# A transformer block with adaptive norms: second norm tile by tile behind the projection, inverse roots by Newton steps on VectorE

## The chip, the cores and the metric

The kernel runs on one core of a Trainium2 chip. The metric is device time in microseconds (us); smaller is better. TensorE is called PE in the profile, VectorE DVE, ScalarE ACT, GpSimd POOL, and the engine that issues most DMAs SP.

## The reference

One block of a transformer over x of 8 x 1024 x 512 in float32, with a condition vector of 512 per batch element:

```python
mod = jax.nn.silu(condition) @ Wada + bada
sh_a, sc_a, gt_a, sh_m, sc_m, gt_m = jnp.split(mod, 6, axis=1)
xn = _layernorm(x, g1, be1)
xm = xn * (1.0 + sc_a[:, None, :]) + sh_a[:, None, :]
x = x + gt_a[:, None, :] * _attention(xm, Wqkv, Wproj, bproj)   # 16 heads, causal
xn = _layernorm(x, g2, be2)
xm = xn * (1.0 + sc_m[:, None, :]) + sh_m[:, None, :]
h = jax.nn.gelu(xm @ W1 + b1, approximate=False)
x = x + gt_m[:, None, :] * (h @ W2 + b2)
```

`_layernorm` takes mean and variance over the 512 features of a row and multiplies by one over the root of the variance plus 1e-5. The hidden layer has 2048 features.

## The kernel before, in words

The 8 x 1024 rows are 16 blocks of 512 rows (two per batch element); a block is four tiles of 128 rows. Each block goes through these steps: norm and modulation ("a"), projections k, q and v, attention in four groups of four heads, output projection with the residual add (`project_out`), norm and modulation ("m"), four `up` steps with GELU, four `down` parts and the second residual add. Products of 512 x 512 are made from seven products of halves (`strassen`), with sums of halves of weights kept in DRAM.

The order of all engines' queues is written out when the kernel is built. A planner keeps one clock per engine (`now`, lines 94 to 141). Each instruction is issued together with a `note` that books its engine for so many ns, and records when its results are due (`written`) and its inputs free (`left`). `linear` walks through the steps of `plan` as one thread of TensorE work, side threads (`start`) run beside it, and attention (`attend`) takes TensorE by turns with them: `step_aside` lets linear work run until the tile that attention needs is due, and `work` advances the thread whose needs are due first. Work of VectorE and ScalarE that can wait stands in lists (`jobs`, `act_jobs`, `pool_jobs`) and is issued when the planner's clocks say that it is due. `either` chooses VectorE or GpSimd for an elementwise operation, `sooner` VectorE or ScalarE.

In PSUM, TensorE has one tile of four banks for scores ("sc", L1541; emptied by VectorE with the mask add L1553 and the row maxima L1556) and for weights of attention ("st", L1620 and L1632; emptied by ScalarE's exponential L1644), a bank for the weighted sum of values ("po", L1672), and three banks for all linear products (L202) and transposes (L735), emptied by VectorE (L193, L185, L739) or ScalarE (L188, L745). GpSimd sums the attention weights (L1762), masks them (L1649) and splits the maxima into bfloat16 parts (L1575 to L1578; VectorE in some cases).

A norm (`normalize`, L580) has four statistics on VectorE (`bn_stats`, `bn_aggr`: L590, L591), booked 850 ns each, and then, once for all four tiles, `power` on GpSimd (L611 to L616): variance plus eps, the power -1/2, and the offset, booked 1500. The normalized tile ("hat") is then made by VectorE or ScalarE (L626, L631). The first two blocks' first norm uses a root on ScalarE and a reciprocal (`root`), and the last block's second norm goes tile by tile through ScalarE (`normalize_tile`). In `project_out` (L1013) the product of each tile is multiplied by the gate row into y (L1044), added to the residual by `add_to` (L1054, issued at L158 on VectorE or L161 on GpSimd), and after the fourth tile `normalize` is called (L1061). `modulated` then transposes the normalized tiles on TensorE (L735) for the keys in `by_pe`, which are a0, a1 and every m; the other keys go through `turn`, by block transposes on VectorE (L671) and DRAM.

Of the kernel before, what the change touches and what calls it, by code (L numbers as in the profile page):

```python
# [8 lines left out]

F32 = mybir.dt.float32  # L10
BF16 = mybir.dt.bfloat16
AF = mybir.ActivationFunctionType
ALU = mybir.AluOpType
AX = mybir.AxisListType
# [3 lines left out]
EPS = 1e-5  # L18
# [4 lines left out]
def kernel(  # L23
# [36 lines left out]
    P = 128  # L60
# [51 lines left out]
    def note(engine, ns, reads=(), writes=(), port=False):  # L112
        start = max(now[engine], due(reads, writes))
        if port:
            start = max([start] + [b for a, b in pool_spans if a <= start < b])
        end = start + ns
        now[engine] = end
        if engine == "POOL":
            pool_spans.append((start, end))
            del pool_spans[:-16]  # L120
        for k in reads:
            left[k] = max(left.get(k, 0.0), end + SYNC)
        for k in writes:
            written[k] = end + SYNC
        return end
# [275 lines left out]
    nc.gpsimd.memset(eps, EPS)  # L401
    ones = const.tile([P, hd], F32, tag="ones", name="ones")
    nc.gpsimd.memset(ones, 1.0)
    minus_half = const.tile([P, NTT], F32, tag="minus_half", name="minus_half")
    nc.gpsimd.memset(minus_half, -0.5)
    minus_ones = const.tile([P, P], BF16, tag="minus_ones", name="minus_ones")
    nc.gpsimd.memset(minus_ones, -1.0)
    mcols = const.tile([P, NTT, P], BF16, tag="mcols", name="mcols")
# [116 lines left out]
    def add_job(job, reads, first=False):  # L525

        at = sum(1 for other in jobs if other[2]) if first else len(jobs)
        jobs.insert(at, (job, reads, first))
# [48 lines left out]

    hats = {}

    def normalize(tiles, key, sources):  # L580

        for t in range(NTT):
            written["hat", key, t] = NEVER
        mv = small.tile([P, NTT, 2], F32, tag="mv", name=f"mv_{key}")
        rstd = small.tile([P, NTT], F32, tag="rstd", name=f"rstd_{key}")
        offset = small.tile([P, NTT], F32, tag="offset", name=f"offset_{key}")

        def statistics(t):
            st = small.tile([P, nc.vector.BN_STATS_DIM], F32, tag="st", name=f"st_{key}_{t}")
            nc.vector.bn_stats(st, tiles[:, t, :])  # L590
            nc.vector.bn_aggr(mv[:, t, :], st)  # L591
            note("DVE", 850, [sources[t]], [("mv", key)])
            if t < NTT - 1:
                return
            if alone[0]:
                root()
                for i in range(NTT):
                    apply_tile(i)
                return
            power()  # L600
            for i in range(NTT):
                act_jobs.append((lambda i=i: apply_tile(i), [("rstd", key)]))

        def root():
            nc.scalar.activation(rstd, mv[:, :, 1], AF.Sqrt, bias=eps)
            note_act(300, "sqrt", [("mv", key)], [("rstd", key)])
            nc.vector.reciprocal(rstd, rstd)
            nc.vector.scalar_tensor_tensor(offset, mv[:, :, 0], -1.0, rstd, ALU.mult, ALU.mult)
            note("DVE", 360, [("rstd", key)], [("rstd", key)], port=True)

        def power():  # L611
            nc.gpsimd.tensor_scalar(rstd, mv[:, :, 1], EPS, None, ALU.add)
            nc.gpsimd.tensor_tensor(rstd, rstd, minus_half, ALU.pow)
            nc.gpsimd.tensor_scalar(offset, mv[:, :, 0], -1.0, None, ALU.mult)
            nc.gpsimd.tensor_tensor(offset, offset, rstd, ALU.mult)
            note("POOL", 1500, [("mv", key)], [("rstd", key)])  # L616

        to = [None]

        def apply_tile(t):  # L620
            if t == 0:
                hats[key] = to[0] = hat_tile(key) if key[0] == "m" else tiles
            xh, xt = to[0][:, t, :], tiles[:, t, :]
            reads, writes = [("rstd", key)], [("hat", key, t)]
            if (key == "a0" and t % 2) if alone[0] else sooner(reads, writes, 700, 800) == "DVE":
                nc.vector.tensor_scalar(  # L626
                    xh, xt, rstd[:, t : t + 1], offset[:, t : t + 1], ALU.mult, ALU.add
                )
                note("DVE", 700, reads, writes, port=True)
            else:  # L630
                nc.scalar.activation(  # L631
                    xh, xt, AF.Identity, bias=offset[:, t : t + 1], scale=rstd[:, t : t + 1]
                )
                note_act(800, None, reads, writes)

        for t in range(NTT):
            add_job(lambda t=t: statistics(t), [sources[t]], key[0] == "m")

    def normalize_tile(xt, key, t, source):

# [22 lines left out]
    def turn(key, rows, xm):  # L663

        small_blocks = xm.rearrange("p c n -> p (c n)")
        by_tile = small_blocks.rearrange("p (m h t i) -> p h m t i", m=NTT, h=NC, t=NTT)
        written["blocks", key] = NEVER

        def turn_tile(t):
            into = by_tile[:, :, :, t, :]  # L670
            nc.vector.transpose(into, rows[:, t, :].rearrange("p (h m i) -> p h m i", m=NTT, i=Q))  # L671
            done = [("blocks", key)] if t == NTT - 1 else []
            note("DVE", 620, [("hat", key, t)], done)

        for t in range(NTT):
            add_job(lambda t=t: turn_tile(t), [("hat", key, t)], key[0] == "m")
        yield [("blocks", key)], []
        held = kept.tile([P, NTT * D], F32, tag=f"held_{turns[0] % 2}", name=f"held_{key}")
        turns[0] += 1
        nc.sync.dma_start(held, small_blocks)  # L680
        written["held", key] = now["PE"] + HOLDING
        yield [("held", key)], []
        for m in range(NTT):
            some = held[:, ts(m, D)].rearrange("(a i) d -> i a d", i=Q)
            nc.sync.dma_start(rows[ts(m, Q), :, :], some)
        written["turned", key] = now["PE"] + HOLDING
        yield [("turned", key)], []
# [4 lines left out]
    def modulated(key, gain, shift, b, guards):  # L692
        for t in ("B11", "B21", "B22", "T1", "T2", "T3", "T4"):
            written[key, t] = NEVER
        turned = key not in by_pe
        if turned:
            yield [*(("hat", key, t) for t in range(NTT)), *guards], []
        else:
            yield [("hat", key, 0), *guards], [BANK]
        got = hats.pop(key)  # L700
# [309 lines left out]
    def add_to(xt, other, reads, writes, op=ALU.add):  # L1010
        either(xt, xt, other, op, [*reads, *writes], writes)

    def project_out(n):  # L1013
        at = take(NC)
        yield [("attended", n), ("xr begun", n)], []
        attT = qTs[n]
        tiles = [residual[n][:, t, :] for t in range(NTT)]
        last = n == NB - 1
        begun = []

        def begin(t):

            bank = yield from accumulate(
                [(attT[:, c, ts(t, P)], piece(at[c])) for c in range(NC - 1)], [("att", n)], False
            )
            begun.append(bank)

        for t, xt in enumerate(tiles):
            if last:
                while len(begun) <= max(t, 1):  # L1030
                    yield from begin(len(begun))
                bank = begun[t]
                yield [("att", n, t)], []
                matmul(
                    banks[bank], attT[:, NC - 1, ts(t, P)], piece(at[NC - 1]), False, True,
                    [("att", n, t)], bank,
                )
            else:
                bank = yield from accumulate(
                    [(attT[:, c, ts(t, P)], piece(at[c])) for c in range(NC)], [("att", n)]  # L1040
                )
            y = tmp.tile([P, D], F32, tag="y", name=f"y_{n}_{t}", bufs=2)
            ky = y_key("proj", True)
            combine_out(y, bank, banks[bank], gate_rows["ga"], [("row", "ga")], [ky], ALU.mult)  # L1044
            if last:
                run_pool_jobs(True)
                nc.vector.tensor_tensor(xt, xt, y, ALU.add)
                note("DVE", 700, [ky, ("xr", n, t)], [("xr", n, t)], port=True)
                following = normalize_tile(xt, f"m{n}", t, ("xr", n, t))
                if t > 0:  # L1050
                    pending()
                pending = following
            else:
                add_to(xt, y, [ky], [("xr", n, t)])  # L1054
        if last:
            pending()
        release(*at)
        run_pool_jobs(True)
        bias_row(n, "m")
        if not last:  # L1060
            normalize(residual[n], f"m{n}", [("xr", n, t) for t in range(NTT)])  # L1061

    def up(step):
        _, n, q = step
# [874 lines left out]
```

## Time and profile before

| | us |
|---|---|
| median of 3 runs | 3546.16 (3545.45 to 3546.95) |
| the profiled execution's own time | 3542.2 |
| its span, first to last instruction | 3540.5 |
| PE busy | 3482.5 (98%) |
| DVE busy | 2174.2 (61%) |
| POOL busy | 2074.9 (59%) |
| ACT busy | 1190.1 (34%) |

The profile is of one execution. Busy times are of each engine's own instructions, waits left out; the mean clock that the throttle granted to TensorE was 0.998 of full. A group row reads: line, engine, operation, output and inputs by the program's names, shapes and count; then busy time, mean ns of one, and the engine's idle time just before, with what ended it. A row of waits reads: who, on whom, total us, times, longest.

### The profile page before, as it was taken

Reading aid. Unit: us, or ns where it says so; the run is one execution under the profiler, and the core shown is the slowest. Engines: PE = TensorE matmul, PEld = TensorE weight load, DVE = VectorE, ACT = ScalarE, POOL = GpSimd, SP = SyncE. Lnnn points to the kernel's source line nnn. Section 1 sums busy time; section 2 is a strip of 40 time slices with the busy share of each in tenths; the row PEclk is TensorE's granted clock in tenths of the full one; section 3 lists DMA queues with packets and bytes.
Section 4 is the critical chain, followed back from the end, with each engine's and each line's share of the span. In section 5 each row is a group of like instructions: output and inputs, shape, how many; then the busy total and the mean of one; then the engine's idle time right before and its main releaser. Section 6 shows DMA issues by size and latency. Waiting matters only on the chain.

```text
span 3540.5 us, 120499 instructions
## 1 busy us (share of the span) xinstructions
PE 3482.5 (98%) x54621; PEld 1738.0 (49%) x54621; DVE 2174.2 (61%) x2383; ACT 1190.1 (34%) x1237; POOL 2074.9 (59%) x2249
## 2 busy tenths in 40 slices
PE   8999999999999999999999999999999999999999
PEld 4444445445554555545554454544545445454445
DVE  5776675564756557565675656656566556655563
ACT  2334323352333513235232342323423234232521
POOL 2667836666376664666546675366762667526660
PEclk9999999999999999999999999999999999999999
DMA  6753434335443354524445334443344533443334
GB/s 198 245 163 103 137 117 140 111 111 156 117 148 103 110 160 117 168 85 126 142 118 159 103 115 141 124 149 107 118 132 127 156 106 119 135 126 124 100 110 140
DMA packets 319555, 465.96 MB, mean 132 GB/s; under 512 B 26300, under 2 KB 176636, under 8 KB 316996
## 3 DMA queue, kind: packets, MB, share of 16 engines
q1 hardware_dynamic: 318928, 458.22, 42.9%
q8 instruction: 430, 7.05, 0.8%
q14 instruction: 81, 0.66, 0.1%
q10 hardware_dynamic: 116, 0.03, 0.0%
HBM read 412.99 MB, written 43.06 MB: 129 GB/s over the span
## 4 chain that ended last, share of the span: by engine, by line
PE 88%; DMA 4%; DVE 3%; POOL 2%; issue 1%; ACT 1%; SPq 0%; ACTq 0%; DVEq 0%; POOLq 0%
PE bank L202 61%; PE sc L1541 8%; PE po L1672 7%; PE st L1632 7%; PE st L1620 3%; DMA w<-in_L_cond_Wproj_dram 2%; PE bank L1693 2%; PE bank L735 1%; DVE mx L1556 1%; POOL pT L1762 1%; DMA w<-in_L_cond_Wada_dram 1%; PE bank L1594 0%; POOL hT L161 0%; POOL xr L161 0%; DVE sc L1553 0%
## 5 line engine op out<-in xcount | busy, mean ns | idle before, releaser
L1762 POOL TENSOR_TENSOR pT<-pT,pT 128x256 f32<-128x256 f32 (+3 forms) x1254 | 1207.2, 998 | 347.9 <-PE po L1672 181.4
L1644 ACT ACTIVATE pT<-st 128x2048 f32<-128x2048 f32 x288 | 541.0, 1879 | 1000.5 <-PE st L1632 883.3
L202 PE MATMUL bank<-w,hT 128*32 128x256 f32 x14336 | 812.3, 380 | 1.1 <-ACT rec L1702 0.9
L1556 DVE TENSOR_REDUCE mx<-sc 128x4 f32<-128x2048 f32 (+3 forms) x384 | 666.0, 1755 | 197.7 <-PE sc L1541 191.6
L202 PEld LDWEIGHTS bank<-w,hT 128*32 128x32 f32 x14336 | 450.4, 110 | 369.2 <-issue 81.4
L202 PE MATMUL bank<-xm_m,w 128*32 128x256 f32 x8192 | 499.6, 381 | 0.0
L202 PE MATMUL bank<-t_m,w 128*32 128x256 f32 x6144 | 381.2, 380 | 0.0
L1649 POOL TENSOR_SCALAR_AFFINE_SELECT pT<-pT 128x512 f32<-128x512 f32 x256 | 168.8, 677 | 346.6 <-ACT pT L1644 344.2
L202 PEld LDWEIGHTS bank<-xm_m,w 128*32 128x32 f32 x8192 | 255.7, 110 | 224.7 <-issue 62.4
L1553 DVE TENSOR_TENSOR sc<-sc,mask 128x1024 f32<-128x1024 f32 (+1 forms) x160 | 162.9, 1018 | 319.7 <-PE sc L1541 242.5
L1541 PE MATMUL sc<-kT,qT 32*128 32x512 f32 (+3 forms) x3072 | 329.1, 520 | 1.8 <-DVE mx L1556 1.1
L1672 PE MATMUL po<-pT,v 128*32 128x512 f32 (+3 forms) x3048 | 302.9, 492 | 2.0 <-POOL pT L1649 2.0
L1632 PE MATMUL st<-qT,kT 32*128 32x512 f32 (+3 forms) x3072 | 301.0, 487 | 0.0
L202 PEld LDWEIGHTS bank<-t_m,w 128*32 128x32 f32 x6144 | 190.0, 110 | 173.3 <-issue 48.5
L202 PE MATMUL bank<-xm_a,w 128*32 128x256 f32 x3968 | 249.3, 382 | 0.0
L202 PE MATMUL bank<-w,qT 128*32 128x512 f32 x2048 | 238.2, 594 | 8.7 <-DMA w<-in_L_cond_Wproj_dram 7.2
L1711 DVE RECIPROCAL rec<-rec 128x128 f32<-128x128 f32 x256 | 225.7, 920 | 31.5 <-ACT rec L1702 31.5
L1541 PEld LDWEIGHTS sc<-kT,qT 32*128 32x128 f32 x3072 | 129.3, 183 | 179.3 <-issue 73.0
L193 DVE TENSOR_TENSOR hT<-bank,u_u 128x512 f32<-128x512 f32 x192 | 129.9, 687 | 114.1 <-PE bank L202 107.4
L202 PE MATMUL bank<-t_a,w 128*32 128x256 f32 x2944 | 188.4, 382 | 0.4 <-ACT xm_m L745 0.4
L1069 ACT ACTIVATE hT<-hT,cols 128x512 f32<-128x512 f32 x256 | 164.4, 711 | 35.5 <-DVE hT L193 35.0
L202 PEld LDWEIGHTS bank<-xm_a,w 128*32 128x32 f32 x3968 | 122.7, 110 | 105.5 <-issue 32.6
(216 smaller groups left out, 3384.6 us busy)
## 6 DMA issues: line engine op xcount, KB each, us to landing
w<-in_L_cond_W_dram SPq DMA_DIRECT2D x384, 256.0 KB
w<-kept_up_S SPq DMA_DIRECT2D x256, 256.0 KB
w<-kept_down_S SPq DMA_DIRECT2D x256, 256.0 KB
w<-kept_qkv_S SPq DMA_DIRECT2D x180, 256.0 KB
w<-in_L_cond_Wqkv_dram SPq DMA_DIRECT2D x147, 256.0 KB
hat_a<-in_x_dram SPq DMA_DIRECT2D x64, 256.0 KB
xr<-in_x_dram SPq DMA_DIRECT2D x32, 512.0 KB
w<-in_L_cond_Wproj_dram SPq DMA_DIRECT2D x64, 256.0 KB
```

The lines of the kernel that those rows point to most:

```text
L193: nc.vector.tensor_tensor(out, src, other, op)
L202: nc.tensor.matmul(ps[r, :], columns, rhs, start=start, stop=stop, skip_group_check=True)
L1069: nc.scalar.activation(hT[:, i, :], hT[:, i, :], AF.Gelu, bias=cols[:, O_B1 + f : O_B1 + f + 1])
L1541: nc.tensor.matmul(sc[:, j, c0 : c0 + w], qTs[n][r, gg, ts(qt, P)], keys_of(n, kh)[r, gg, :w], start=True, stop=True, skip_group_check=True,)
L1553: nc.vector.tensor_tensor(place, place, shape_of.to_broadcast(place.shape), ALU.add)
L1556: nc.vector.tensor_reduce(maxima[n, gg][:, kh, qt, :], sc[:, :, c0 : c0 + w], axis=AX.X, op=ALU.max)
L1632: nc.tensor.matmul(st[:, j, c0 : c0 + w], kT[r, gg, ts(k % NTT, P)], qT[r, gg, TB - w :], start=False, stop=True, skip_group_check=True,)
L1644: nc.scalar.activation(pT[:, :, :used], st[:, :, :used], AF.Exp, scale=scale)
L1649: nc.gpsimd.affine_select(diagonal, diagonal, pattern=[[0, HPG], [1, P]], compare_op=ALU.is_ge, fill=0.0, base=0, channel_multiplier=-1,)
L1672: nc.tensor.matmul(po[r, TB - w :], v[:, k % NTT, g * P + j * hd : g * P + (j + 1) * hd], pT[:, j, c0 : c0 + w], start=(k == 0), stop=last ...
L1711: nc.vector.reciprocal(some, some)
L1762: nc.gpsimd.tensor_tensor(into, into, pT[:, j, c0 : c0 + w], ALU.add)
```

## The change

It makes one over the root of the variance on VectorE: a first guess from the bits of the half variance (shift, subtract from a constant) and three Newton steps of three instructions each (`inverse_root`); the offset is one more instruction. `power` of the first norm calls this for four tiles at once. In `project_out` (all blocks but the last) the residual add is always on VectorE, and right behind it stand the tile's statistics; after the second and the fourth tile follow the root and the offset for the pair, and the two normalized tiles are put into the list for ScalarE and VectorE. The pending adds of `pool_jobs` are issued ahead of the projection and no longer behind it. `modulated` and `turn` get a branch for turned keys that begin with m.

```diff
+    GUESS = float(0x5F3759DF - (1 << 22)) - 2.0**31
+    def inverse_root(out, variance, key):
+        size = [P, out.shape[1]]
+        half_of = small.tile(size, F32, tag=f"half{size[1]}", name=f"half_{key}")
+        square = small.tile(size, F32, tag=f"square{size[1]}", name=f"square_{key}")
+        nc.vector.tensor_scalar(half_of, variance, EPS, 0.5, ALU.add, ALU.mult)
+        bits = out.bitcast(I32)
+        nc.vector.tensor_scalar(bits, half_of.bitcast(I32), 1, None, ALU.logical_shift_right)
+        nc.vector.tensor_scalar(bits, bits, -1.0, GUESS, ALU.mult, ALU.add)
+        for _ in range(3):
+            nc.vector.tensor_tensor(square, out, out, ALU.mult)
+            nc.vector.tensor_tensor(square, square, half_of, ALU.mult)
+            nc.vector.scalar_tensor_tensor(out, square, 1.5, out, ALU.subtract, ALU.mult)
...
         def power():
-            nc.gpsimd.tensor_scalar(rstd, mv[:, :, 1], EPS, None, ALU.add)
-            nc.gpsimd.tensor_tensor(rstd, rstd, minus_half, ALU.pow)
-            nc.gpsimd.tensor_scalar(offset, mv[:, :, 0], -1.0, None, ALU.mult)
-            nc.gpsimd.tensor_tensor(offset, offset, rstd, ALU.mult)
-            note("POOL", 1500, [("mv", key)], [("rstd", key)])
+            inverse_root(rstd, mv[:, :, 1], key)
+            nc.vector.scalar_tensor_tensor(offset, mv[:, :, 0], -1.0, rstd, ALU.mult, ALU.mult)
+            note("DVE", 1000, [("mv", key)], [("rstd", key)], port=True)
...
+    def statistics_at_once(tiles, key, t, source, kept_of={}):
+        pair = t // 2
+        if t % 2 == 0:
+            kept_of[key, pair] = small.tile([P, 2, 2], F32, tag=f"mv{pair}", name=f"mv_{key}_{pair}")
+        mv = kept_of[key, pair]
+        st = small.tile([P, nc.vector.BN_STATS_DIM], F32, tag="st", name=f"st_{key}_{t}")
+        nc.vector.bn_stats(st, tiles[:, t, :])
+        nc.vector.bn_aggr(mv[:, t % 2, :], st)
+        note("DVE", 850, [source], [("mv", key)], port=True)
+        if t % 2 == 0:
+            return
+        rstd = small.tile([P, 2], F32, tag=f"rstd{pair}", name=f"rstd_{key}_{pair}")
+        offset = small.tile([P, 2], F32, tag=f"offset{pair}", name=f"offset_{key}_{pair}")
+        inverse_root(rstd, mv[:, :, 1], f"{key}_{pair}")
+        nc.vector.scalar_tensor_tensor(offset, mv[:, :, 0], -1.0, rstd, ALU.mult, ALU.mult)
+        note("DVE", 1000, [("mv", key)], [("rstd", key, pair)], port=True)
+        def apply(i):
...
+            if sooner(reads, writes, 700, 800) == "DVE":
+                nc.vector.tensor_scalar(xh, xt, rstd[:, by], offset[:, by], ALU.mult, ALU.add)
...
+            else:
+                nc.scalar.activation(xh, xt, AF.Identity, bias=offset[:, by], scale=rstd[:, by])
...
+        for i in (t - 1, t):
+            act_jobs.append((lambda i=i: apply(i), [("rstd", key, pair)]))
...
         for t in range(NTT):
-            add_job(lambda t=t: turn_tile(t), [("hat", key, t)], key[0] == "m")
+            if key[0] == "m":
+                yield [("hat", key, t)], []
+                turn_tile(t)
+            else:
+                add_job(lambda t=t: turn_tile(t), [("hat", key, t)])
...
         turned = key not in by_pe
-        if turned:
+        if turned and key[0] == "a":
             yield [*(("hat", key, t) for t in range(NTT)), *guards], []
+        elif turned:
+            yield [("hat", key, 0), *guards], []
...
         last = n == NB - 1
+        run_pool_jobs(True)
+        for t in range(NTT):
+            written["hat", f"m{n}", t] = NEVER
...
             else:
-                add_to(xt, y, [ky], [("xr", n, t)])
+                nc.vector.tensor_tensor(xt, xt, y, ALU.add)
+                note("DVE", 700, [ky, ("xr", n, t)], [("xr", n, t)], port=True)
+                statistics_at_once(residual[n], f"m{n}", t, ("xr", n, t))
         if last:
             pending()
         release(*at)
-        run_pool_jobs(True)
         bias_row(n, "m")
-        if not last:
-            normalize(residual[n], f"m{n}", [("xr", n, t) for t in range(NTT)])
```

More of the change, by code (lines that the diff above doesn't have):

```diff
@@ L11 @@
 BF16 = mybir.dt.bfloat16
+I32 = mybir.dt.int32
 AF = mybir.ActivationFunctionType
@@ L403 @@
     nc.gpsimd.memset(ones, 1.0)
-    minus_half = const.tile([P, NTT], F32, tag="minus_half", name="minus_half")
-    nc.gpsimd.memset(minus_half, -0.5)
     minus_ones = const.tile([P, P], BF16, tag="minus_ones", name="minus_ones")
@@ L637, in normalize @@
             add_job(lambda t=t: statistics(t), [sources[t]], key[0] == "m")
+    def statistics_at_once(tiles, key, t, source, kept_of={}):
[15 more added lines that the diff above has]
+        def apply(i):
+            if i == 0:
+                kept_of[key] = hats[key] = hat_tile(key)
+            xh, xt = kept_of[key][:, i, :], tiles[:, i, :]
+            by = slice(i % 2, i % 2 + 1)
+            reads, writes = [("rstd", key, pair)], [("hat", key, i)]
+            if sooner(reads, writes, 700, 800) == "DVE":
+                nc.vector.tensor_scalar(xh, xt, rstd[:, by], offset[:, by], ALU.mult, ALU.add)
+                note("DVE", 700, reads, writes, port=True)
+            else:
+                nc.scalar.activation(xh, xt, AF.Identity, bias=offset[:, by], scale=rstd[:, by])
+                note_act(800, None, reads, writes)
+        for i in (t - 1, t):
+            act_jobs.append((lambda i=i: apply(i), [("rstd", key, pair)]))
     def normalize_tile(xt, key, t, source):
```

## The prediction

> **What bounds the kernel now.** I read the page first, then the stages, then the waits of TensorE. The page gives the span and the busy times:
>
> ```profile
> span 3540.5 us, 120499 instructions
> PE 3482.5 (98%) x54621; PEld 1738.0 (49%) x54621; DVE 2174.2 (61%) x2383; ACT 1190.1 (34%) x1237; POOL 2074.9 (59%) x2249
> PE 88%; DMA 4%; DVE 3%; POOL 2%; issue 1%; ACT 1%; SPq 0%; ACTq 0%; DVEq 0%; POOLq 0%
> ```
>
> TensorE is busy for 98% of the span and holds 88% of the chain that ended last. The view of busy time by stage, for the stretch without start and end (columns: stretch, length, then PE, PEld, DVE, ACT, POOL), says how much is left to gain there:
>
> ```profile
> 300.00:3400.00 3100.00, 3077.68 (x48036) 1531.07 (x48032) 1898.38 (x2037) 1071.91 (x1099) 1884.37 (x2035) 1.00 0.42 126
> ```
>
> In 3100 us TensorE idles 22.3 us. The change adds and removes no matmul, so the most that it could gain here is some 22 us, 0.6%. The waits of TensorE (who waited for whom: total, times, longest) name what these are:
>
> ```profile
> PE st L1620 <- DVE mx L1556: 7.4, 6, 2.4
> PE bank L202 <- DMA w<-in_L_cond_Wproj_dram: 7.2, 9, 1.5
> ...
> PE bank L1594 <- POOL mcols L1578: 3.9, 3, 1.6
> ...
> PE po L1672 <- POOL pT L1649: 2.0, 1, 2.0
> PE bank L1594 <- DVE y_d L193: 1.8, 1, 1.8
> PE bank L1594 <- DVE mcols L1578: 1.6, 2, 1.3
> ...
> PE sc L1541 <- DVE mx L1556: 1.1, 1, 1.1
> ```
>
> The reader is to see that GpSimd ends only 5.9 us of waits, while VectorE ends 11.9 us in these rows alone. VectorE empties the PSUM tiles that TensorE needs next, and it does so in the order of its queue. So the question is not how much work moves but whether VectorE comes late.
>
> **The change, part by part.** *Removed from GpSimd:* the roots of both norms (L612 to L615) and the residual adds behind the projection. Columns of the next rows: count, busy, mean ns, idle before.
>
> ```profile
> L613 POOL TENSOR_TENSOR rstd_m<-rstd_m,minus_half 128x4 f32<-128x4 f32 x15 | 15.7, 1047 | 1.2
> L613 POOL TENSOR_TENSOR rstd_a<-rstd_a,minus_half 128x4 f32<-128x4 f32 x14 | 15.5, 1106 | 1.2
> L614 POOL TENSOR_SCALAR offset_m<-mv_m 128x4 f32<-128x4 f32 x15 | 3.6, 238 | 1.0
> L161 POOL TENSOR_TENSOR xr<-xr,y 128x512 f32<-128x512 f32 x41 | 52.6, 1286 | 112.0 <-DVE y L193 111.9
> ```
>
> With three small operations of about 0.24 each beside a power of 1.05 to 1.11 us, 29 roots make 29 x 1.8 = 52 us, and the adds 52.6: GpSimd loses 105 us of 2075, and 111.9 us in which it stood waiting for y. It is off the path, so I credit only its part of TensorE's waits, 5.9 us, and of that 4.
>
> *Added to VectorE:* `inverse_root` is 12 instructions (three tensor_scalar, then three rounds of three), and the offset makes 13. The first norm runs it 14 times, the second twice per block for 15 blocks: 44 chains, 572 instructions, each on 2 or 4 elements per partition and each reading what the one before wrote. They stand in one piece in VectorE's queue; no PSUM tile is emptied between them. The script books 1.0 us for a whole chain (`note("DVE", 1000, ...)`), and the order of all engines is written out on that footing. No row shows the chain itself; its nearest rows bound it. From below, two dependent small operations in the tail, where GpSimd is quiet:
>
> ```profile
> 3427.82 0.13 DVE L653 RECIPROCAL rstd_m<-rstd_m 128x1 f32<-128x1 f32 x1
> 3427.99 0.16 DVE L654 SCALAR_TENSOR_TENSOR offset_m<-mv_m,rstd_m 128x1 f32<-128x1 f32 x1
> ```
>
> One step is 0.17 us, so 13 x 0.17 = 2.2 us. From above, four small operations on VectorE while GpSimd runs adds (timelines of the two engines):
>
> ```profile
> 396.34 0.88 DVE L1575 CAST mcols<-mx 128x16 bf16<-128x16 f32 x1
> 397.26 1.17 DVE L1576 TENSOR_TENSOR rest<-mx,mcols 128x16 f32<-128x16 f32 x1
> 398.54 1.16 DVE L1577 CAST mcols<-rest 128x16 bf16<-128x16 f32 x1
> 399.73 1.23 DVE L1578 TENSOR_TENSOR mcols<-rest,mcols 128x16 bf16<-128x16 f32 x1
> ```
> ```profile
> 395.89 4.98 POOL L1762 TENSOR_TENSOR pT<-pT,pT 128x512 f32<-128x512 f32 x4
> ```
>
> Each took about as long as one of GpSimd's adds (4.98 / 4 = 1.25). At 1.18 us per step a starved chain lasts 13 x 1.18 = 15.3 us. Between the ends lies the average of single small operations, and of GpSimd's adds:
>
> ```profile
> L1570 DVE TENSOR_TENSOR mx<-mx 128x16 f32<-128x16 f32 x32 | 18.6, 581 | 0.6
> ```
> ```profile
> L1762 POOL TENSOR_TENSOR pT<-pT,pT 128x256 f32<-128x256 f32 (+3 forms) x1254 | 1207.2, 998 | 347.9 <-PE po L1672 181.4
> ```
>
> L1570 averages 0.58 us where 0.17 would do: such waits are common. The adds take 1207.2 us for 1254, 0.96 us each, so a chain that runs beside adds of the usual mix all the way lasts 13 x 0.96 = 12.5 us; that is the upper end that I use, since 15.3 needs the widest adds alone.
>
> [...]
>
> *Where the chains stand.* For the first norm I took seven stretches of 12 us that begin at the fourth statistics of a block:
>
> ```profile
> 536.00:548.00 12.00, 12.00 (x204) 6.34 (x200) 7.37 (x8) 7.08 (x13) 11.68 (x18) 1.00 0.37 112
> ...
> sum 84.00, PE 84.00 PEld 43.80 DVE 63.35 ACT 47.39 POOL 76.44; mean PE 12.00 PEld 6.26 DVE 9.05 ACT 6.77 POOL 10.92
> ```
>
> GpSimd is busy for 10.9 of 12 us there, so chains of the first norm will mostly run beside adds. I take the middle of 2.2 and 12.5, some 7 us: 6 us late against the booked 1.0. What takes lateness up is VectorE's own idle time ahead of score tiles:
>
> ```profile
> DVE sc L1553 <- PE sc L1541: 242.5, 118, 12.2
> DVE mx L1556 <- PE sc L1541: 191.6, 113, 6.5
> ```
>
> That is 434.1 us over 231 waits, 1.9 us each. Two of them leave 6 - 3.8 = 2.2 us, which reaches TensorE: 14 x 2.2 = **31 us**.
>
> For the second norm the stage is the projection, three blocks of which I measured, the last one shown with the sum:
>
> ```profile
> 2371.00:2395.00 24.00, 24.00 (x268) 8.02 (x260) 12.68 (x14) 5.55 (x6) 13.71 (x17) 1.00 0.26 78
> sum 72.00, PE 72.00 PEld 24.20 DVE 38.70 ACT 18.00 POOL 41.22; mean PE 24.00 PEld 8.07 DVE 12.90 ACT 6.00 POOL 13.74
> ```
> ```profile
> 2371.23 1.28 POOL L161 TENSOR_TENSOR xr<-xr,y 128x512 f32<-128x512 f32 x1 [1.75 <-DVE y L193]
> ...
> 2379.15 3.23 POOL L1762 TENSOR_TENSOR pT<-pT,pT 128x256 f32<-128x256 f32 x4
> 2383.29 1.28 POOL L161 TENSOR_TENSOR xr<-xr,y 128x512 f32<-128x512 f32 x1 [0.91 <-DVE y L193]
> 2390.47 1.28 POOL L161 TENSOR_TENSOR xr<-xr,y 128x512 f32<-128x512 f32 x1 [5.91 <-DVE y L193]
> ```
> ```profile
> L590 DVE BATCH_NORM_STATS2 st_m<-xr 128x6 f32<-128x512 f32 x60 | 40.1, 668 | 0.4 <-POOL xr L161 0.4
> L591 DVE BATCH_NORM_AGGREGATE mv_m<-st_m 128x2 f32<-128x6 f32 x60 | 10.9, 182 | 2.1
> L158 DVE TENSOR_TENSOR xr<-xr,y 128x512 f32<-128x512 f32 x19 | 20.2, 1064 | 0.6
> ```
>
> VectorE has 12.9 of 24 us to do there. The change brings four statistics forward into it, 4 x 0.85 = 3.4 us, and the three adds that GpSimd had in the stretch shown, 3 x 0.7 = 2.1 (1.06 if held, as the 19 on VectorE were). The first chain of a block follows the second tile, where GpSimd still has a run of 256-wide adds: say two steps of 0.73, 3.3 us; the second follows the fourth tile, where GpSimd had stood idle 5.9 us: 2.2 us. In all 12.9 + 3.4 + 2.1 + 5.5 = 23.9 of 24 us: it just fits, with no idle time left to absorb anything. Against the booked 2.0 the two chains are 3.5 us late, less one 1.9: 1.6, rounded down to 1.5, for 15 blocks **22 us**. What waits behind a chain is the next reduction of scores (L1556) or emptying of a bank (L193), and behind these TensorE's next tile in the same PSUM; also the transposes at L735, which need the normalized tiles of the second pair.
>
> *At nothing:* the added wait of the normalized tile for the pair's root, because the first pair is done two projection tiles early; emptying of GpSimd's pending adds before the projection instead of after (`run_pool_jobs(True)`), because the loads that they wait for were issued a window earlier, and if that cover were gone GpSimd would stand for a DMA, at most a few us per block; the edits in `turn` and `modulated` for keys that begin with m, because every such key is in `by_pe` and takes the other branch; the two programs' SP queues hold the same DMAs, some twenty rows of them in another place, and the weights that come late now (7.2 us in the row above) stay as late. TensorE's order has 1270 changes of matmul shape in place of 1283, which at the script's own 150 ns (L99) is 2 us, and I leave it out.
>
> **Sum:** 31 + 22 - 4 = +49 us on the profiled execution's own time of 3542.2 (span 3540.5 and 1.7 around it): 3591. The median of the runs, 3546.16, lies 4.0 above that execution, so I predict **3595 us**.
>
> **The rivals.** *Starved throughout:* GpSimd's adds slide beside every chain. First norm 12.5 - 1.0 - 3.8 = 7.7 x 14 = 108 us; second norm, each chain meeting four held steps (2.2 + 4 x 0.79 = 5.4), 15 x (10.8 - 2 - 1.9) = 104: +212, 3758. For it: 91% busy GpSimd; against it: the projection stage, where GpSimd idles, and 105 us less work for it. *Hidden:* GpSimd sits still during chains, each is 1.2 us late and the 1.9 us of idle takes it: 0 to +15, 3546 to 3561. [...] Against it: L1570's mean. *Faster:* chains stay under 1.0 + 1.9 = 2.9 us, so nothing new is late, and GpSimd, rid of 105 us and of its waits for y, delivers sooner: at most the 5.9 us that it ends and, with VectorE's 11.9 if the new order suits them, 17.8; I price it at -10, 3536. It decides at 2.9 us per chain. That the change would not do what it says I see no way: the order of the changed program shows the 13 instructions on VectorE, 44 times, and no power on GpSimd.
>
> **How the numbers follow.** Forecast (+20 to +110): 0.53. Starved (beyond +110): 0.12. Hidden: 0.22, half of it within 0.2%. Faster: 0.13. A measurement of this kernel can tell about 0.2%, 7 us, from no change. So faster 0.13, same 0.11, slower 0.76. The range that should hold it 8 times in 10 runs from 3541, which leaves out most of the faster case, to 3660, which leaves out most of the starved one; the forecast's own is 3566 to 3656.
>
> **What would show it.** Chains of 13 that last 2.2 us beside a quiet GpSimd and 7 or more beside its adds; VectorE's busy time up by some 200 us (14 x 7 + 30 x 2.75 = 180, and the adds); TensorE's idle between 300 and 3400 us up from 22 to about 70, with L1620, L1541 and L735 waiting for VectorE's reductions and normalized tiles. Wrong if chains stay near 2.2 us everywhere, or if they last 7 and TensorE does not wait: then idle time took up more than 1.9 us per score tile.

## The result, and the profile after

The changed kernel takes 3656.47 us (median of four runs, 3654.63 to 3663.32), the kernel before 3545.80 beside it (3543.54 to 3546.95). The ratio is 1.0316, 95% interval 1.0299 to 1.0334: **110.7 us slower**. The prediction said 3595, so the direction is right and the size less than half. The profiled execution took 3663.32 us, the slowest of the four.

The page of the changed kernel, first the span, the busy times and the chain that ended last; then the mean clock that was granted to TensorE, after and before:

```profile
span 3661.5 us, 120974 instructions
PE 3523.2 (96%) x54621; PEld 1747.4 (48%) x54621; DVE 2347.6 (64%) x2974; ACT 1206.7 (33%) x1258; POOL 1971.0 (54%) x2092
PE 75%; DVE 9%; DMA 3%; POOL 2%; issue 1%; ACT 1%; SPq 0%; DVEq 0%; ACTq 0%; POOLq 0%
```
```profile
core 0: 3661.5 us, clock 0.986
```
```profile
core 0: 3540.5 us, clock 0.998
```

Three things are to be seen. TensorE has the same 54621 matmuls, but its idle time (span less busy) went from 58.0 to 138.3 us, +80.3. Its busy time went up too, from 3482.5 to 3523.2, **+40.7 us for the same matmuls**. Together that is the whole 121.0 by which the span grew. And VectorE's share of the last chain went from 3% to 9%.

The second part is the clock: (1 - 0.986) x 3661.5 = 51 us of full clock are missing, before (1 - 0.998) x 3540.5 = 7. Step by step, the trace has 20 stretches at half clock after, 99 us in all, and 3 of 13.7 us before (one at the very end of each is left out). Half of the difference is 42.7 us, about the 40.7 of added busy time.

The view by stage for the middle (as shown of before) and TensorE's waits on other engines:

```profile
300.00:3400.00 3100.00, 3005.62 (x46428) 1486.86 (x46428) 2005.70 (x2547) 1033.35 (x1068) 1710.48 (x1815) 0.99 0.42 122
```
```profile
PE st L1675 <- DVE mx L1611: 39.6, 21, 4.3
PE sc L1596 <- DVE mx L1611: 21.2, 14, 7.8
PE bank L788 <- ACT hat_m L680: 11.2, 10, 5.3
...
PE bank L203 <- DVE u_u L194: 5.1, 2, 4.9
```

Idle time in these 3100 us is 94.4 in place of 22.3. L1611 is the reduction of the scores that was L1556; the wait of "st" on it went from 7.4 to 39.6 us, that of "sc" from 1.1 to 21.2, with a longest of 7.8. The third row is the transposes (L735 before) waiting for normalized tiles.

The 13 instructions themselves, grouped by shape on VectorE (columns: count, busy us, mean ns, idle before). The last row is one that is never held:

```profile
L591 DVE TENSOR_TENSOR square_m<-rstd_m 128x2 f32<-128x2 f32 x90 | 20.3, 225 | 3.1
...
L593 DVE SCALAR_TENSOR_TENSOR rstd_a<-square_a,rstd_a 128x4 f32<-128x4 f32 x42 | 16.2, 385 | 1.4
...
L589 DVE TENSOR_SCALAR rstd_m<-rstd_m 128x2 int32<-128x2 int32 x30 | 11.3, 375 | 1.0
L660 DVE BATCH_NORM_AGGREGATE mv_m<-st_m 128x2 f32<-128x6 f32 x60 | 10.9, 182 | 2.0
```

Means hide two kinds. Here are the first and last instruction of a chain of the first norm while GpSimd was still, then of one that ran beside GpSimd's adds, with what stood behind it in VectorE's queue; then GpSimd's and TensorE's rows for the second:

```profile
1269.74 0.17 DVE L586 TENSOR_SCALAR half_a<-mv_a 128x4 f32<-128x4 f32 x1
...
1272.13 0.16 DVE L628 SCALAR_TENSOR_TENSOR offset_a<-mv_a,rstd_a 128x4 f32<-128x4 f32 x1
```
```profile
1028.25 0.61 DVE L586 TENSOR_SCALAR half_a<-mv_a 128x4 f32<-128x4 f32 x1
...
1030.96 0.94 DVE L592 TENSOR_TENSOR square_a<-square_a,half_a 128x4 f32<-128x4 f32 x1
...
1036.43 1.19 DVE L628 SCALAR_TENSOR_TENSOR offset_a<-mv_a,rstd_a 128x4 f32<-128x4 f32 x1
1037.53 2.28 DVE L1611 TENSOR_REDUCE mx<-sc 128x4 f32<-128x2048 f32 x1
```
```profile
1028.11 8.27 POOL L1817 TENSOR_TENSOR pT<-pT,pT 128x256 f32<-128x256 f32 x12
```
```profile
1039.87 2.09 PE L1596 MATMUL sc<-kT,qT 32*128 32x512 f32 x8 [7.85 <-DVE mx L1611]
```

The same 13 instructions take 1272.13 + 0.16 - 1269.74 = 2.55 us alone and 9.37 beside GpSimd's adds, twelve of 0.69 us each and wider ones behind them. In the second case the reduction L1611 stands behind the chain, and TensorE, which needs its PSUM tile, idles 7.85 us. What follows is seen in the stretches around it (the column before the last two is the clock):

```profile
1028.00:1032.00 4.00, 4.00 (x61) 1.77 (x56) 3.76 (x7) 3.88 (x6) 4.00 (x7) 1.00 0.14 33
1032.00:1040.00 8.00, 0.15 (x7) 0.14 (x4) 7.76 (x10) 2.35 (x4) 8.00 (x11) 0.73 0.16 56
1040.00:1044.00 4.00, 4.00 (x28) 1.37 (x32) 2.38 (x2) 0.57 (x1) 1.26 (x2) 0.50 0.02 4
1044.00:1048.00 4.00, 4.00 (x60) 2.07 (x56) 0.70 (x2) 0.59 (x1) 0.00 (x0) 0.75 0.27 65
```

After the wait TensorE is busy again at once, but at half clock for four microseconds and more. In the busy column this looks like full work; only the clock column shows it.

Over the whole trace, the 14 chains of the first norm last 2.54 to 9.36 us, 69.4 in all (mean 4.96); the 30 of the second 2.53 to 8.36, 104.8 in all (mean 3.82 for the first pair of a block, 3.17 for the second). Waits of TensorE that fall in a chain or up to 14 us behind it sum up to 75.4 us, most of the 80.3.

### The profile page after: what moved, and what is told of

Its sections match the earlier page's. It is cut to its first block, busy times and chain, and to the rows that moved or that the text cites. A ratio compares the mean times of both kernels' runs of the same rounds, so it can differ in the third digit from the quotient of the medians.

```text
span 3661.5 us, 120974 instructions
## 1 busy us (share of the span) xinstructions
PE 3523.2 (96%) x54621; PEld 1747.4 (48%) x54621; DVE 2347.6 (64%) x2974; ACT 1206.7 (33%) x1258; POOL 1971.0 (54%) x2092
## 4 chain that ended last, share of the span: by engine, by line
PE 75%; DVE 9%; DMA 3%; POOL 2%; issue 1%; ACT 1%; SPq 0%; DVEq 0%; ACTq 0%; POOLq 0%
PE bank L203 51%; PE sc L1596 7%; PE po L1727 6%; PE st L1687 6%; PE st L1675 2%; DMA w<-in_L_cond_Wproj_dram 2%; DVE mx L1611 2%; PE bank L1748 1%; PE bank L788 1%; POOL pT L1817 1%; DVE xr L1110 1%; POOL hT L162 1%; DVE y L194 1%; DVE st_m L659 1%; DVE sc L1608 0%
## 5 line engine op out<-in xcount | busy, mean ns | idle before, releaser
L1611 DVE TENSOR_REDUCE mx<-sc 128x4 f32<-128x2048 f32 (+3 forms) x384 | 665.7, 1754 | 166.7 <-PE sc L1596 160.5
L1596 PE MATMUL sc<-kT,qT 32*128 32x512 f32 (+3 forms) x3072 | 333.7, 525 | 28.3 <-DVE mx L1611 21.2
L1687 PE MATMUL st<-qT,kT 32*128 32x512 f32 (+3 forms) x3072 | 309.0, 498 | 0.0
L203 PE MATMUL bank<-w,qT 128*32 128x512 f32 x2048 | 236.4, 596 | 10.2 <-DMA w<-in_L_cond_Wproj_dram 10.1
L1596 PEld LDWEIGHTS sc<-kT,qT 32*128 32x128 f32 x3072 | 130.6, 184 | 197.5 <-ACT pT L1699 70.3
```

Of the source, the lines that this page charges most:

```text
L203: nc.tensor.matmul(ps[r, :], columns, rhs, start=start, stop=stop, skip_group_check=True)
L1596: nc.tensor.matmul(sc[:, j, c0 : c0 + w], qTs[n][r, gg, ts(qt, P)], keys_of(n, kh)[r, gg, :w], start=True, stop=True, skip_group_check=True,)
L1611: nc.vector.tensor_reduce(maxima[n, gg][:, kh, qt, :], sc[:, :, c0 : c0 + w], axis=AX.X, op=ALU.max)
L1687: nc.tensor.matmul(st[:, j, c0 : c0 + w], kT[r, gg, ts(k % NTT, P)], qT[r, gg, TB - w :], start=False, stop=True, skip_group_check=True,)
```

## The experiments

The theory after the result: a chain stands in one piece in VectorE's queue, GpSimd's adds hold it, and the reduction or emptying behind it makes TensorE wait, with a stretch at half clock as a second price. The rivals: the new order of the second norm costs by itself; or the planner's booking of 1.0 us for a chain is what hurts, and an honest booking would put the chains where they cost nothing. Each kernel is compared with the kernel before on the same chip (3543.1 to 3544.1 us).

**No Newton step, and six.** Same order of TensorE, ScalarE and GpSimd as the changed kernel, with chains of 4 and of 22 instructions (the edit of the second is `range(6)`). Neither makes the proper root: the guess is negative and each step flips its sign.

```diff
-        for _ in range(3):
+        for _ in range(0):
```

> The changed kernel without its Newton steps: the root is only the first guess from the bits (so the norm is off by some per cent); 4 instructions per chain in place of 13, and the order of all queues is that of the changed kernel. Theory A (a chain lasts longer than the booked 1.0 us, VectorE comes late, TensorE waits, and each wait also drops its clock to half for some us): chains of about 1 us, no lateness, few half-clock stretches, 3545 to 3575 us. Rival B (the new order itself costs it: adds and statistics on VectorE inside the projection): stays at 3630 or more. Rival C (VectorE's total load): 130 us less of 2348 busy, so some 60% of the loss goes, about 3590.

> The changed kernel with six Newton steps in place of three, same order, 22 instructions per chain. A: chains 1.9 us longer beside a quiet GpSimd and more beside its adds, 90 to 130 us of further lateness in 44 chains, nearly all of which reaches TensorE now that the idle time is used up, and half as much again by the half clock: 3770 to 3850 us. B: no more than 3680. C: VectorE's load up by 150 us of busy time, 3680 to 3750.

Measured: 3557.79 us, ratio 1.0041 (1.0027 to 1.0055), +14.3; and 3772.93, ratio 1.0648 (1.0632 to 1.0663), +229.5. Both lie in the ranges of theory A, the second at its low end, and outside those of B and C. The chains sum up to 58.6 us and 275.9 (the changed kernel: 174.2). With no step TensorE's wait for the reductions is nearly as before the change:

```profile
PE st L1675 <- DVE mx L1611: 7.4, 10, 3.2
...
PE sc L1596 <- DVE mx L1611: 3.4, 5, 1.3
```

So neither the order of the second norm nor its adds on VectorE make the 111 us: at the changed kernel's own order, all of it but the Newton steps costs 14.3. At a given order, the time rises with the time of the chains; the table below shows how evenly.

**One norm alone.** The first norm's root on VectorE in the kernel before (the edit is against that kernel); and the changed kernel with the first norm's root back on GpSimd.

```diff
-        def power():
+        def power_on_pool():
...
+        def power():
+            if key[0] == "m":
+                return power_on_pool()
+            inverse_root(rstd, mv[:, :, 1], key)
...
```
```diff
...
-            inverse_root(rstd, mv[:, :, 1], key)
-            nc.vector.scalar_tensor_tensor(offset, mv[:, :, 0], -1.0, rstd, ALU.mult, ALU.mult)
-            note("DVE", 1000, [("mv", key)], [("rstd", key)], port=True)
+            nc.gpsimd.tensor_scalar(rstd, mv[:, :, 1], EPS, None, ALU.add)
+            nc.gpsimd.tensor_tensor(rstd, rstd, minus_half, ALU.pow)
...
```

> The kernel before with the first norm's root alone on VectorE (14 chains), the second norm as before. A: the five or six chains that fall beside GpSimd's adds cost 4 to 8 us each and their half clock: 3570 to 3600. B: nothing of the projection changes, 3546 to 3556. C: VectorE's load up by 70 us, a fifth of the loss, about 3565.

> The changed kernel with the first norm's root back on GpSimd; second norm tile by tile with its 30 chains on VectorE. A: without the long chains of the first norm 40 to 55 us less than the changed kernel: 3600 to 3616. B: 3640 to 3656. C: about 3635.

Measured: 3598.94, ratio 1.0157 (1.0142 to 1.0172), +55.5 for the first norm; 3613.10, ratio 1.0196 (1.0181 to 1.0211), +69.7 for the second. Both lie at the upper end of theory A's ranges, and the other theories' are missed. The sum of 125 is a little over the 111 of both, so the parts nearly add. In the traces the first norm's part is 37.8 us of idle time and 20.5 lost to half clock, the second's 54.1 and 15.4 (half of the length of the stretches at half clock, less that of before).

**Booked as long as they are.** The changed kernel with the 13 instructions booked 200 ns each, each put off to the end of the GpSimd instruction that the planner has there; and with fixed sums near the measured means.

```diff
-            note("DVE", 1000, [("mv", key)], [("rstd", key)], port=True)
+            for _ in range(12):
+                note("DVE", 200, port=True)
+            note("DVE", 200, [("mv", key)], [("rstd", key)], port=True)
...
```
```diff
-            note("DVE", 1000, [("mv", key)], [("rstd", key)], port=True)
+            note("DVE", 5000, [("mv", key)], [("rstd", key)], port=True)
...
-        note("DVE", 1000, [("mv", key)], [("rstd", key, pair)], port=True)
+        note("DVE", 3500, [("mv", key)], [("rstd", key, pair)], port=True)
```

> The changed kernel with each of a chain's 13 instructions booked by itself, 200 ns and not beside a GpSimd instruction that the planner has booked (port), in place of 1.0 us for the chain; what is computed is the same, the queues are ordered anew. Theory A (it is the time that was not booked that makes VectorE late): TensorE's waits for VectorE and the half clock go for the most part, 3555 to 3600 us. Rival D (VectorE cannot do this work in time wherever it stands): 3630 or more.

> The changed kernel with a chain booked at its measured mean: 5.0 us for the first norm, 3.5 for a pair. A: most of the waits go, 3555 to 3600 us; somewhat less than with each step booked if the long chains beside adds are what is left. D: 3630 or more.

Measured: 3627.58, ratio 1.0235 (1.0219 to 1.0250), +83.5; and 3637.78, ratio 1.0262 (1.0247 to 1.0278), +93.7. The first lies between theory A and rival D, the second in D's range. An honest booking gives back 17 to 27 us of 111, and that I had thought it could give back most was wrong. The planner moved the chains, but to places with more adds: those of the first norm went from 69.4 us in all to 85.3 and 95.9, and TensorE's idle time only from 138.3 to 120.6 and 133.3. It learns how long a chain is, and still can put nothing inside it.

**The pair's root on GpSimd.** The changed kernel with its statistics tile by tile and adds on VectorE, and both norms' roots by the power on GpSimd. The planner orders the queues anew, so this isn't the changed kernel's order.

```diff
...
-        inverse_root(rstd, mv[:, :, 1], f"{key}_{pair}")
-        nc.vector.scalar_tensor_tensor(offset, mv[:, :, 0], -1.0, rstd, ALU.mult, ALU.mult)
-        note("DVE", 1000, [("mv", key)], [("rstd", key, pair)], port=True)
+        nc.gpsimd.tensor_scalar(rstd, mv[:, :, 1], EPS, None, ALU.add)
+        nc.gpsimd.tensor_tensor(rstd, rstd, minus_half[:, :2], ALU.pow)
...
+        note("POOL", 1500, [("mv", key)], [("rstd", key, pair)])
```

> Second norm tile by tile behind the projection, adds and statistics on VectorE as in the changed kernel, but each pair's root on GpSimd by the power, and the first norm's root there too: the change without its Newton steps. A: 3545 to 3565 us, as the run with 4 instructions per chain. Rival B (the adds and statistics inside the projection cost it): 3590 or more. If tile by tile is a gain by itself: below 3540.

Measured: 3569.45, ratio 1.0072 (1.0055 to 1.0089), +25.3. That is 4 us above theory A's range and far below rival B's. The second norm alone, with each pair's root on VectorE, cost 69.7, so its chains account for some 44 of these. The other 25 stand without any chain on VectorE, but they can't be put down to the new place of the norm as such: in the changed kernel's own order four-instruction chains and the new place together cost only 14.3. The order that the planner chose here and the power behind each pair are in these 25 too, and no run separates them. The clock is 0.997 to 0.999 over the four executions, 0.999 in the profiled one, so it is as before.

**Thirteen instructions that nothing holds.** The order of the changed kernel; each chain is ten `bn_aggr`, two memsets and the offset. The root is left out (it is 1).

```diff
...
+        scratch = small.tile([P, 6], F32, tag="scratch", name=f"half_{key}")
+        nc.vector.memset(scratch, 1.0)
+        for _ in range(10):
+            nc.vector.bn_aggr(scratch[:, 0:2], scratch)
+        nc.vector.memset(out, 1.0)
```

> The changed kernel's order, with chains of 13 instructions that GpSimd does not hold up: ten bn_aggr on six elements, two memsets that set the root to 1, and the offset; the root is left out. Chains of 2.2 to 2.5 us each, 44 x 2.4 = 105 us in all in place of 174. A with a cost that grows with the chains' total (14 us at 59, 112 at 174 us): about +55, 3585 to 3610 us. Rival E (only chains held up by GpSimd cost anything, 2.5 us is taken up by idle time): 3545 to 3570. Rival F (the count of instructions decides): about 3650.

Measured: 3580.89, ratio 1.0103 (1.0088 to 1.0118), +36.8. That is under theory A's range and over rival E's, so neither is right as it stood, and F is wrong. The groups of this kernel show that each `bn_aggr` kept its length (a mean of 182 ns over all 440), also in chains that run beside GpSimd's adds:

```profile
L586 DVE BATCH_NORM_AGGREGATE half_m<-half_m 128x2 f32<-128x6 f32 x300 | 54.6, 182 | 10.4
L586 DVE BATCH_NORM_AGGREGATE half_a<-half_a 128x2 f32<-128x6 f32 x140 | 25.5, 182 | 4.9
```

All 44 chains now last 2.43 to 3.15 us, 111.7 in all. The queues of TensorE, ScalarE and GpSimd are those of the changed kernel and VectorE has as many instructions in each chain; what is gone is 62.5 us of holding, and with it 111 - 37 = 74 us. **Two thirds of the loss are GpSimd's holds.** This is the experiment that tells most: it leaves the order and the count alone, and nearly the length of a chain that isn't held (2.43 and 2.53 us). GpSimd itself is busy for 1967.9 us here and for 1971.0 in the changed kernel, so it isn't a slower GpSimd that costs.

**In pieces, and with two steps.** The 13 instructions cut into five pieces in VectorE's list, each instruction booked as in the first of the two bookings above, so that an emptying can go between them (`guess` is L586 to L589, `newton` L591 to L593, `last` the offset and the tiles to normalize); the changed kernel with two steps in place of three, the guess positive, since two steps flip its sign twice; and both.

```diff
...
+        add_job(guess, [("mv", key)], True)
+        for _ in range(3):
+            add_job(newton, [("mv", key)], True)
+        add_job(last, [("mv", key)], True)
...
```
```diff
-    GUESS = float(0x5F3759DF - (1 << 22)) - 2.0**31
+    GUESS = float(0x5F3759DF - (1 << 22)) 
...
-        for _ in range(3):
+        for _ in range(2):
```

> The changed kernel, its 13 instructions cut into five pieces (guess, three Newton steps, offset) that stand in VectorE's list one by one, each instruction booked 200 ns as in e5_book_each (3627.6). The planner can put emptyings of PSUM between the pieces. Theory 1, what costs is that the chain stands in one piece ahead of the emptyings and reductions that TensorE waits for: the wait behind a chain shrinks from the whole chain to one piece, some 2 us beside GpSimd's adds, and TensorE's waits for the reductions (39 us of rows over L1615 in e5) fall under half: 3580 to 3600. Theory 2, what costs is VectorE's time as such, held by GpSimd, wherever it stands: 3615 to 3635, as e5. Theory 3, the normalized tiles come later still, as the chain's pieces wait their turn, and TensorE's transposes wait for them: over 3640.

> The changed kernel with two Newton steps in place of three (10 instructions to a chain, positive guess, order of TensorE, ScalarE and GpSimd as in the changed kernel). Chain free of GpSimd: 2.53 x 10/13, 1.95 us. Theory 1, the cost goes with the chain's whole time: between no steps (58.6 us of chains, +14) and three (174.2, +112) some 136 us and +65 to +85: 3609 to 3629. Theory 2, chains under some 2 us cost nothing and only held ones do: 3580 to 3600.

> Pieces as in e9_pieces with two Newton steps: the most of both. Theory 1 (one piece costs): 3565 to 3585. Theory 2 (VectorE's time as such): 3590 to 3610. Below 3546, faster than before, by neither.

Measured: in pieces 3586.69, ratio 1.0119 (1.0101 to 1.0137), +43.6; two steps in one piece 3621.87, ratio 1.0224 (1.0205 to 1.0242), +78.8; both 3589.49, ratio 1.0130 (1.0114 to 1.0146), +46.4. TensorE's waits for the reductions, first with the same booking in one piece, then in pieces:

```profile
PE st L1679 <- DVE mx L1615: 20.5, 20, 3.8
PE sc L1600 <- DVE mx L1615: 18.3, 6, 5.2
```
```profile
PE st L1691 <- DVE mx L1627: 16.1, 14, 2.6
...
PE bank L804 <- DVE hat_m L690: 8.6, 1, 8.6
PE sc L1612 <- DVE mx L1627: 6.6, 7, 2.9
```

They fall from 38.8 to 22.7, not to under half as I had expected, but the long ones are gone (5.2 to 2.9), and the time falls by 41 us, into theory 1's range, although a chain of the first norm now takes 11.1 us from first to last instruction on average. Nor does the later root show in TensorE's waits for normalized tiles: one of 8.6 us (L804), against 8.8 us in two with the chain in one piece. That it is the block in the queue that costs, this run alone doesn't show, since the pieces also meet fewer adds: the 572 instructions take 172.2 us of VectorE's time in one piece with this booking, and 135.5 in pieces. Two steps in one piece say more. They take 123.4 us of VectorE's time and cost 78.8; the pieces take 135.5 and cost 43.6. The orders differ, but if VectorE's time as such were what costs, it would be the other way round. Two steps in one piece also lie within the +65 to +85 of the theory that counts the chain's whole time (137 us here). Both edits together do no better than pieces alone, and come out between what the two theories expected, so that run tells neither apart: what is left, some 44 us, no longer falls with the number of instructions. The wait of 8.6 us is in it, and what the new place of the second norm costs; the rest I haven't separated. No version with roots on VectorE comes to the time of the kernel before.

At the changed kernel's order of TensorE's queue the runs line up like this (the last two columns are from each run's one profiled execution):

| chain | all 44 chains, us | time over before, us | TensorE idle, us | lost to half clock, us |
|---|---|---|---|---|
| 4 instructions | 58.6 | +14.3 | 65.9 | 11.9 |
| 13, never held | 111.7 | +36.8 | 85.5 | 15.4 |
| 10 | 137.0 | +78.8 | 111.9 | 32.4 |
| 13 (the change) | 174.2 | +110.7 | 138.3 | 49.5 |
| 22 | 275.9 | +229.5 | 219.9 | 100.7 |

Lost to half clock is half of the length of the stretches at half clock in the trace, the one at the very end left out; before it was 6.8, and idle 57.9. TensorE also idles in such stretches (for some 4 of the changed kernel's one of 10.2 us), so the column is an upper bound. From the first row to the last, 217 us of chain cost 215 us, and TensorE's busy time rises by 63.0 (3489.3 to 3552.3). But that a microsecond of chain costs a microsecond of kernel holds between these ends alone. From the first row to the second, where no chain lasts over 3.2 us, 53 us of chain cost 22.5; a straight line from four instructions to thirteen would have had the second row at +59, not +36.8. Long blocks cost more than their share.

## Why the prediction was right in direction and wrong in size

*What bounds the kernel: right.* TensorE, with VectorE's queue as what it waits for.

*The chain's length: nearly right at both ends, and averaged in between.* Forecast 2.2 us alone and 7 and more beside adds; measured 2.53, and up to 9.4. The step of 0.17 us was read from two instructions of one element; thirteen in a row take 0.195 each. The mean for the first norm is 4.96 and not 7, since six of the 14 chains found GpSimd still throughout. VectorE's busy time rose by 2347.6 - 2174.2 = 173 us against some 200.

*First norm, 14 x 2.2 = 31 us: right as waiting time by luck, wrong as a time.* Waits at chains of the first norm sum up to 30.4 us in the trace. But they are not 14 of 2.2: five chains have 4.2 to 7.9 us each, three have 0.3 to 2.8, and six have none. Two errors cancel here. The mean chain was put too long, and too much was taken off it: with the measured mean the prediction's own working would leave 4.96 - 1.0 - 3.8 = 0.2 us per chain, 2 us in all, while the chain of 9.36 us shown above left a wait of 7.85. Behind each of the five long ones stands a stretch at half clock of 6.8 to 10.2 us. Alone, this part costs 55.5.

*The step that failed first: a wait was priced at its own length.* Every term of the sum, "which reaches TensorE", ends with the idle time and has no term for what the clock does afterwards. That missing term is 40.7 us of busy time in the page's two lines, a third of the 121.0 by which the span grew; the idle time itself was forecast at 53, less the credit of 4, and rose by 80.3. It could have been seen in the trace of before: its waits of 2.01 and 2.41 us at 111.9 and 219.1 us stand ahead of stretches of 3.4 us at half clock (two more, of 2.66 and 2.04 us, don't), but the stage that I read has the clock at 1.00.

*The step that failed second: the second norm's 22 us, which measured 69.7 alone* (54.1 of idle time and 15.4 lost to half clock). Its chains were forecast at 3.3 and 2.2 us, 5.5 per block, and measured 3.8 and 3.2, 7.0: the part that isn't held is 2 x 2.53 and not 2 x 2.2, and the holds are 1.9 and not 1.1. Since 3.9 of the 5.5 were taken off, 1.5 us more doubles what is left: with the measured chains the same working gives 7.0 - 2.0 - 1.9 = 3.1 per block, 46 us, and 45 are seen as waits. So the length of the chains is the term that was mis-sized. "Less one 1.9" stands in contradiction with the prediction's own 23.9 of 24 us for this stage, which leaves no idle time; the number comes out with it, but no run shows that VectorE's idle time took up 1.9. "At nothing" for the placing isn't borne out either: all but the Newton steps costs 14.3 at the changed kernel's order, four-instruction chains included.

*The credit of 4 us for GpSimd:* no run shows it. GpSimd lost the 104 us of work that were forecast (2074.9 to 1971.0), and the time didn't follow.

*The rivals.* "Hidden" had chains of 2.2 us, 1.2 late, with all of it taken up by idle time. The thirteen that nothing holds are such chains (2.5 us), and they cost 36.8, not 0 to 15. Less the 14.3 of the run with four instructions that is still 22.5, so it is wrong even without GpSimd's holds. Only chains of four instructions (1.3 us, 0.3 over the booking) come out in its range, at 14.3. "Faster" let everything under 2.9 us go free, and fails by the same run. The thirteen don't fit into the booked 1.0 us even beside a still GpSimd: the chain shown above has 0.16 to 0.17 us per instruction and 0.03 to 0.04 between them, 2.55 in all. "Starved throughout" had the mechanism of the long chains, but only nine of the 44 last over 5 us. The result lies just inside the range, 3.5 us from its end, and 0.5 us beyond the forecast's own 3566 to 3656.

*What would show it:* L1620 and L1541 (now L1675 and L1596) lead the list of waits as forecast, and the transposes come third; idle from 300 to 3400 us is 94 and not 70.

*Still open:* why the run with the pair's root on GpSimd costs 25 us with no chain on VectorE (after the first 30 us it has 54 waits of TensorE between 0.3 and 1 us, 29 us in all, against 16 with 10 before); what the new place of the second norm costs in the changed kernel's own order, where 14.3 bounds it together with short chains; and what else is in the 44 us that the pieces leave.

## What to carry to other kernels

Price a run of small dependent instructions by its longest cases beside the other engine (9.36 us here) and not by the mean (4.96): it is the block in the queue, and what stands behind it, that TensorE meets. If such work has to go on the engine that empties PSUM, put it in pieces into the list, so that emptyings can go between; with each instruction booked, that gave 41 us more here, where the booking by itself gave 27. And a wait of TensorE may cost more than itself (here 11 of 12 waits from 2.04 to 2.79 us had 3.4 us at half clock behind them): look at the clock column of the stretch behind it.

## What the runs showed of the hardware

*A wait of 2 us can cost clock.* After the first 30 us of the changed kernel, TensorE had 13 waits of 1.0 to 1.7 us with no stretch at half clock behind them; of 12 waits from 2.04 to 2.79 us, 11 were followed by one of 3.4 us; all nine from 3.2 us on were, eight of them by 6.8 us or more (one wait of 1.0 us just ahead of another of 3.2 is left out, and the one at the very end). The other traces are less clear-cut. Over all thirteen, taking waits of TensorE with no other of 1 us or more within 4 us, a stretch at half clock followed 6 of 161 waits of 1 to 2 us, 60 of 90 of 2 to 3 us, and 65 of 66 longer ones. Of the changed kernel's 20 stretches twelve last 3.4 us, seven 6.8 and one 10.2.

*Which small instructions were held.* Beside GpSimd's adds an instruction with one input was held as well as one with two: in the rows above L586 takes 0.61 us in place of 0.17, and L592 0.94 where it takes 0.16 alone; L589 has a mean of 375 ns for the pairs. `bn_aggr` was not held: all 128 of the changed kernel's norms take 181 to 184 ns, the 38 that ran wholly beside GpSimd's adds 181 to 183, and the 440 of the thirteen that nothing holds have a mean of 182.
